# A four-layer image kernel: the first reading in the text's order with spread row transforms, blocks evicted by one engine, logarithms ahead of squares

## The chip, the cores and the metric

The kernel runs on one core of one Trainium2 chip. The metric is the device time of one execution in microseconds (us). Before the change, three executions took 5182.60, 5175.65 and 5182.61 us, the median being 5182.6. One more execution was recorded by the hardware profiler; its own time is in the table below. Engines are named as in the profile: PE is the matrix engine TensorE, DVE is VectorE, ACT is ScalarE, POOL is GpSimd, SP is SyncE, which only issues DMAs here.

## What is computed

An image x of 256 x 256 pixels and 128 channels (float32) goes through four residual layers. Each first normalises x over pixels and groups of four channels:

```
x = x + L0(_gn(x))    # attention along rows, 4 heads of 32, with a pair bias
x = x + L1(_gn(x))    # gated recurrence, 16 steps, with spectra of 7x7 kernels
x = x + L2(_gn(x))    # triangle multiplication
x = x + L3(_gn(x))    # 3x3 convolution, then a dense layer

def _gn(v, G=32, eps=1e-5):
    g = v.reshape(B_, H_, W_, G, C_ // G)
    m = jnp.mean(g, axis=(1, 2, 4), keepdims=True)
    s = jnp.var(g, axis=(1, 2, 4), keepdims=True)
    return ((g - m) / jnp.sqrt(s + eps)).reshape(v.shape)
```

The mean of the first `_gn` is over the whole image, so the image has to be read once before anything else can be done with it. L0 and L2 then apply a layer norm over the channels of each pixel: `(z - mu) * rsqrt(mean((z - mu)**2) + 1e-5)`. L1 needs `fft2` of two sets of 64 complex kernels of 7 x 7, padded to 256 x 256; it is made as a transform of the rows, then of the columns.

## The kernel before

The work is staged layer by layer, on tiles of up to 128 partitions. Three places concern the change.

**The first reading** (`statistics`, L200 to L273). The image is read in 32 blocks of 1 MB. Blocks 6 to 31 come first, through three rotating buffers `xin`; blocks 0 to 5 come last and stay in SBUF as `kept`, for the next stage. Each block has two halves b. For each, DVE subtracts a shift (`xs`, L244), ACT squares the result (`sqx`, L54 for all activations), and PE adds up `xs` and the square of the half before (`add_up`, tile `acc`, four matmuls of 32 columns in four column groups of the array; L60 for all matmuls). `xs` and `sqx` have two buffers each. In between stands work that the statistics do not need: the attention's weights (`attention_weights`, a generator that is advanced twice), and the row transforms of the recurrence's kernels (`kernel_rows`). `spectrum(g)`, called for g = 0 to 15 at blocks 5 to 20, makes eight small matmuls `ph` with 21 rows of weights, and an ACT copy into `H` (L189). After the eighth and the sixteenth call, eight copies `HH<-H` (L196) follow, four on ACT and four on POOL, and two DMAs of 448 KB issued by SP (`HD<-HH`, L197). `H` has one buffer. Here the tile scheduler orders the instructions on each engine; nothing is pinned to the order of the text.

**The turn/normalise loop** (`attention`, L376 to L473), one block of 2048 pixels at a time, every instruction pinned to the text's order (`keep_in_program_order`). `turn(m)` transposes the block in 16 PE transposes, eight for each half, into PSUM tiles `pt`, and copies each half into `xo` (L391 to L393): ACT takes pixels 0 to 3 of each group of eight, DVE pixels 4 to 7. `centre(m, b)` multiplies by the centring matrix (`zc`), adds a bias on DVE (`zs`), squares on ACT (`sq`). `variance(m)` is a mean by PE (`var`), then Ln and Exp on ACT (`rs`). `normalise(m)` spreads `rs` by PE (`pr`), multiplies on DVE, scales on POOL and stores by a POOL DMA. `pair_bias(m)` is a matmul, a DVE copy `bi` and small DMAs. `pt`, `zc` and `pr` share three PSUM buffers.

**The first loop of the triangle** (`triangle`, L1107 to L1149) does the same layer norm on the output of L1, without the turn. Its order is pinned as well. In each iteration: load, `centre(m+1, 0)` with its square, variance of m, `centre(m+1, 1)` with its square, spread, two products on DVE, two POOL instructions, one store. `zc` and `pr` share three PSUM buffers; `zs` and `sq` have four buffers each, `xin` and `zn` three.

All x tiles are loaded by SP, in its order; stores are issued by POOL.

Of the kernel before, what the change touches and what calls it, by code (L numbers as in the profile page):

```python
# [9 lines left out]
F32 = mybir.dt.float32  # L10
AF = mybir.ActivationFunctionType
# [6 lines left out]
P = 128  # L18
# [4 lines left out]
KS = 7  # L23
# [7 lines left out]
class Kernel:  # L31
# [133 lines left out]
    def kernel_rows(self, sp, ps, HD_):  # L165


        nc, I = self.nc, self.i
        CG = HC // 4
        tu = self.load(sp, I["c_rows"], "tu")  # L170
        HH = sp.tile([P, N // 2, HC], F32, name="HH")
        H, ka = [], []
        for n, (re, im) in enumerate((("A_real", "A_imag"), ("B_real", "B_imag"))):
            kr, ki = (I["L1_conv_" + y].rearrange("c p q -> p c q") for y in (re, im))
            k = sp.tile([3 * KS, HC, 32], F32, name=f"ka{n}")
            nc.gpsimd.memset(k, 0.0)
            for p0, q0, src in ((0, 0, kr), (0, KS, ki), (KS, 0, ki), (2 * KS, KS, kr)):
                nc.gpsimd.dma_start(k[p0:p0 + KS, :, q0:q0 + KS], src)
            ka.append(k)

        def spectrum(g):
            n, g0 = divmod(2 * g, CG)
            if not g0:
                H.append(sp.tile([P, N, CG], F32, name="H"))
            ph = ps.tile([P, 2, N], F32, name="ph", bufs=2)
            for j in range(2):
                for k in range(4):
                    self.mm(ph[32 * k:32 * k + 32, j], ka[n][:, CG * k + g0 + j, :], tu)
            nc.scalar.copy(H[n][:, :, g0:g0 + 2].rearrange("q u c -> q c u"), ph)  # L189
            if g0 + 2 == CG:  # L190
                for h in range(2):
                    o = slice(64 * n + 32 * h, 64 * n + 32 * h + 2 * KS)
                    u = slice(h * N // 2, (h + 1) * N // 2)
                    for k in range(4):
                        copy = nc.gpsimd.tensor_copy if h else nc.scalar.copy
                        copy(HH[o, :, CG * k:CG * (k + 1)], H[n][32 * k:32 * k + 2 * KS, u])  # L196
                    nc.sync.dma_start(HD_[n][:, u], HH[o])  # L197
        return spectrum

    def statistics(self, wp, weights, HD_, kept, src):  # L200

        nc, I = self.nc, self.i
        V = nc.vector
        x = I["x"].rearrange("b h w c -> (b h w) c")
        NM, KEPT = NPIX // 2048, len(kept)
        mv = wp.tile([P, 2], F32, name="mvx")
        with ExitStack() as c:
            sp = c.enter_context(self.pool(name="sp", bufs=1))  # L210
            io = c.enter_context(self.pool(name="p0", bufs=2))
            ps = c.enter_context(self.pool(name="p0s", bufs=1, space=PSUM))
            row = sp.tile([1, P], F32, name="row")
            nc.sync.dma_start(row, x[0:1])
            shc = self.column(sp, x[0:1].rearrange("o c -> (o c)"), "shc")
            ones = sp.tile([P, P], F32, name="ones0")
            V.memset(ones, 1.0)
            psh = ps.tile([P, 4, P], F32, name="psh", tag="ph", bufs=2)
            self.mm(psh[:, 0], ones[0:1], row)
            sh = sp.tile([P, P], F32, name="sh")  # L220
            V.tensor_copy(sh, psh[:, 0])
            acc = ps.tile([P, 512], F32, name="acc")
            last, count = None, [0, 0]

            def add_up(*pair):
                for h in range(2):
                    for j, t in enumerate(pair):
                        if t is not None:
                            o = 64 * j + 32 * h
                            self.mm(acc[o:o + 32], ones[:, :32], t[:, h * 512:(h + 1) * 512],  # L230
                                    start=count[j] < 2, stop=count[j] >= 4 * NM - 2)
                            count[j] += 1

            order = list(range(KEPT, NM)) + list(range(KEPT))
            spectrum = None
            for n, m in enumerate(order):
                if m < KEPT:
                    xin = kept[m]
                else:
                    xin = io.tile([P, 2, 1024], F32, name="xin", bufs=3)  # L240
                nc.sync.dma_start(xin, src(m))
                for b in range(2):
                    xs = io.tile([P, 1024], F32, name="xs")
                    V.tensor_tensor(xs.rearrange("p (t c) -> p t c", t=8), xin[:, b].rearrange("p (t c) -> p t c", t=8),  # L244
                                    sh.unsqueeze(1).to_broadcast([P, 8, P]), ALU.subtract)
                    sq = io.tile([P, 1024], F32, name="sqx")
                    self.act(sq, xs, AF.Square)

                    add_up(xs, last)
                    last = sq  # L250
                if n == 2:
                    spectrum = self.kernel_rows(sp, ps, HD_)
                    next(weights)
                elif 5 <= n < 21:
                    spectrum(n - 5)
                elif n == 23:
                    weights = next(weights)
            add_up(None, last)
            accs = sp.tile([P, 512], F32, name="accs")
            V.tensor_copy(accs, acc)  # L260
            sel = sp.tile([P, 2], F32, name="sel")
            V.memset(sel, 0.0)
            V.memset(sel[:64, 0:1], 1.0 / 32 / NPIX)
            V.memset(sel[64:, 1:2], 1.0 / 32 / NPIX)
            pm = ps.tile([P, 2], F32, name="pmx")
            for t in range(4):
                self.mm(pm, accs[:, t * P:(t + 1) * P], sel, start=t == 0, stop=t == 3)
            V.tensor_copy(mv, pm)
            e = sp.tile([P, 1], F32, name="ex")
            V.tensor_tensor(e, mv[:, 0:1], mv[:, 0:1], ALU.mult)  # L270
            V.tensor_tensor(mv[:, 1:2], mv[:, 1:2], e, ALU.subtract)
            V.tensor_tensor(mv[:, 0:1], mv[:, 0:1], shc, ALU.add)
        return mv, weights  # L273
# [59 lines left out]
    def attention(self, wp, later, xT, x1T, znT, biasD, HD_, stats1, shift1):  # L333
# [5 lines left out]
        with ExitStack() as c:  # L339
# [43 lines left out]
            def turn(m):  # L383
                if m >= NM:
                    return
                load(m + 2)
                xo[m] = io.tile([P, 2, P, 8], F32, name="xo")
                for b in range(2):
                    pt = wide("pt").rearrange("c (t p) -> c t p", t=8)
                    for t in range(8):  # L390
                        transpose(pt[:, t], xin[m][:, b, t * P:(t + 1) * P], self.ident)  # L391
                    for h, f in enumerate((acopy, copy)):
                        f(xo[m][:, b, :, 4 * h:4 * h + 4], pt[:, 4 * h:4 * h + 4].rearrange("c t p -> c p t"))  # L393
                nc.gpsimd.dma_start(xT[:, m * 2048:(m + 1) * 2048], xo[m].rearrange("c b p t -> c (b p t)"))

            def centre(m, b):
# [652 lines left out]
    def triangle(self, x2T, x3T, znT, prodD, stats2, shift2, stats3, prepare):  # L1049
# [12 lines left out]
        with ExitStack() as c:  # L1062
# [47 lines left out]
            with ExitStack() as c1:  # L1110
# [10 lines left out]
                def centre(m, b):  # L1121
                    if m >= NB // 2:
                        return
                    zc = ps.tile([P, 1024], F32, name="zc", tag="w")
                    for k in range(2):
                        s = b * 1024 + k * 512
                        mm(zc[:, k * 512:(k + 1) * 512], lc, xin[m][:, s:s + 512])
                    zs[m, b] = work.tile([P, 1024], F32, name="zs")
                    add(zs[m, b], zc, cb)
                    sq[m, b] = work.tile([P, 1024], F32, name="sq")  # L1130
                    act(sq[m, b], zs[m, b], AF.Square)

                table(LN_EXP)
                for m in range(2):
                    load(m)
                centre(0, 0)
                centre(0, 1)
                for m in range(NB // 2):
                    load(m + 2)
                    centre(m + 1, 0)  # L1140
                    rs = variance(ps, work, [sq[m, b] for b in range(2)])
                    centre(m + 1, 1)
                    pr = spreads(ps, rs)
                    zn = io.tile([P, 2048], F32, name="zn")
                    for b in range(2):
                        z = zn[:, b * 1024:(b + 1) * 1024]
                        tt(z, zs[m, b], pr[b], MUL)
                        nc.gpsimd.tensor_scalar(z, z, lnw, lnb, MUL, ADD)
                    nc.gpsimd.dma_start(znT[:, m * 2048:(m + 1) * 2048], zn)  # L1149
# [398 lines left out]
```

## Time and profile before

| what | value |
|---|---|
| time of the profiled execution | 5189.0 us |
| its span | 5187.2 us, 78333 instructions |
| median of the three runs | 5182.6 us |
| PE busy | 4965.6 us (96%) |
| DVE busy | 4108.0 us (79%) |
| ACT busy | 3518.2 us (68%) |
| POOL busy | 427.6 us (8%) |
| mean granted PE clock | 0.983 |
| moved by DMA | 782.5 MB, mean 151 GB/s |
| first reading, to the first `xT` store | 0 to 181.8 us |
| turn/normalise loop | to about 490 us |
| triangle, first loop | 3284 to 3516 us |

The profile gives for each engine how long it was busy, for the span cut in 40 slices how busy (in tenths), and for groups of instructions their number, mean duration and the idle time ahead of them with its releaser. The timeline lists instructions in order of time: start, duration, engine, line, operation, output and inputs, count, and in brackets how long the engine had been idle and what ended that. PEclk is the clock granted to PE as a share of the full one.

### The profile page before, as it was taken

How to read it: one execution, taken by the hardware profiler on the slowest of the kernel's cores; microseconds unless marked ns; L12 is line 12 of the kernel's file. 1: busy time of each engine (PE TensorE's matmuls, PEld its weight loads, DVE VectorE, ACT ScalarE, POOL GpSimd, SP SyncE). 2: the span in 40 equal slices, each digit the busy share in tenths (PEclk: the TensorE clock that was granted, in tenths of full speed). 3: DMA queues.
4: the chain of work that ended last, by engine and by line, in shares of the span. 5: the costliest groups of instructions: out<-in, count | busy, mean ns of one | idle time of the engine just before them, and what ended most of it. 6: DMA issues, size and time to landing. Idle time of an engine off the chain costs nothing.

```text
span 5187.2 us, 78333 instructions
## 1 busy us (share of the span) xinstructions
PE 4965.6 (96%) x31357; PEld 2702.8 (52%) x31357; DVE 4108.0 (79%) x4829; ACT 3518.2 (68%) x4988; POOL 427.6 (8%) x600
## 2 busy tenths in 40 slices
PE   7899999999999899999999999889999989989999
PEld 1343555555555333333333333228999953339999
DVE  4666999999999799999999999665334527779886
ACT  5444888888888799999999999443333347762110
POOL 2132000000000000000000000240110010000000
PEclk7999999999999899999999999999999999999999
DMA  6797222222222222222222221677667768865432
GB/s 192 275 334 264 73 84 78 86 86 82 79 86 86 63 66 71 69 72 67 71 71 66 71 67 66 243 284 268 230 230 255 244 244 333 323 238 188 144 120 66
DMA packets 180093, 782.47 MB, mean 151 GB/s; under 512 B 31696, under 2 KB 35102, under 8 KB 130518
## 3 DMA queue, kind: packets, MB, share of 16 engines
q1 hardware_dynamic: 122366, 508.44, 29.5%
q0 software_dynamic: 56064, 268.58, 13.9%
q8 instruction: 250, 4.10, 0.3%
q14 instruction: 117, 0.96, 0.1%
q10 hardware_dynamic: 1296, 0.40, 0.0%
HBM read 505.99 MB, written 271.32 MB: 150 GB/s over the span
## 4 chain that ended last, share of the span: by engine, by line
PE 53%; DVE 29%; issue 5%; ACT 2%; POOL 0%; DMA 0%; SPq 0%; POOLq 0%; DVEq 0%; ACTq 0%
PE z L60 9%; PE m L60 7%; PE nd L60 7%; PE sc L60 5%; PE po L60 4%; DVE tr L896 3%; DVE t L893 3%; DVE y L893 3%; DVE p L893 3%; DVE yf L893 3%; PE ppq L60 3%; PE ppv L60 2%; PE zc L60 2%; PE px L60 2%; PE pe L60 2%
## 5 line engine op out<-in xcount | busy, mean ns | idle before, releaser
L561 DVE TENSOR_TENSOR e<-sc,bT 128x1024 f32<-128x1024 f32 x512 | 603.1, 1220 | 49.7 <-PE sc L60 48.8
L54 ACT ACTIVATE e<-e 128x1024 f32<-128x1024 f32 x512 | 540.4, 1055 | 61.5 <-DVE e L561 52.4
L1056 DVE TENSOR_TENSOR LR<-z,sg 128x512 f32<-128x512 f32 x256 | 268.2, 1049 | 368.2 <-ACT sg L54 360.4
L60 PE MATMUL m<-U,v 128*128 128x128 f32 x4608 | 517.6, 276 | 6.6 <-DVE v L1397 6.6
L60 PEld LDWEIGHTS m<-U,v 128*128 128x128 f32 x4608 | 517.4, 193 | 6.7 <-DVE v L1397 6.7
L60 PE MATMUL z<-wf,zt 128*128 128x128 f32 x4096 | 461.7, 276 | 4.0 <-DVE LR L1056 2.7
L60 PEld LDWEIGHTS z<-wf,zt 128*128 128x128 f32 x4096 | 461.3, 193 | 5.2 <-DVE LR L1056 2.9
L54 ACT ACTIVATE sq<-zs 128x1024 f32<-128x1024 f32 x192 | 203.0, 1057 | 284.5 <-DVE zs L371 157.7
L54 ACT ACTIVATE sg<-z 128x512 f32<-128x512 f32 x256 | 153.0, 598 | 312.4 <-PE z L60 308.6
L561 DVE TENSOR_TENSOR ks<-e 128x1024 f32<-128x1024 f32 x256 | 301.0, 1217 | 0.0
L60 PE MATMUL sc<-tq,tk 32*128 32x256 f32 x4096 | 297.2, 401 | 2.8 <-DVE e L561 1.9
L60 PE MATMUL nd<-e,tv 128*32 128x256 f32 x4096 | 271.9, 383 | 0.0
L60 PEld LDWEIGHTS sc<-tq,tk 32*128 32x128 f32 x4096 | 186.6, 184 | 159.5 <-issue 96.3
L54 ACT ACTIVATE dn<-dn 128x512 f32<-128x512 f32 x384 | 241.9, 630 | 13.3 <-DVE dn L561 2.6
L60 PE MATMUL av<-y,ident 128*128 128x512 f32 x384 | 192.2, 610 | 44.0 <-DVE y L893 44.0
L60 PE MATMUL po<-LR 128*128 128x256 f32 x1024 | 222.2, 380 | 7.0 <-DVE LR L1056 7.0
L1434 ACT COPY m4s<-m 128x512 f32<-128x512 f32 x32 | 18.7, 585 | 287.3 <-PE m L60 287.3
L60 PEld LDWEIGHTS po<-LR 128*128 128x128 f32 x1024 | 194.1, 190 | 34.2 <-DVE LR L1056 7.7
L60 PE MATMUL bx<-p,ident 128*128 128x512 f32 x384 | 192.3, 610 | 0.0
L54 ACT ACTIVATE o<-po 128x256 f32<-128x256 f32 x256 | 84.3, 381 | 145.3 <-issue 111.6
L60 PEld LDWEIGHTS nd<-e,tv 128*32 128x32 f32 x4096 | 120.2, 110 | 109.8 <-issue 44.2
L864 ACT ACT_TABLE_LOAD x132 | 169.4, 1283 | 1.5
(369 smaller groups left out, 10376.8 us busy)
## 6 DMA issues: line engine op xcount, KB each, us to landing
zt<-znT SPq DMA_DIRECT2D x128, 1024.0 KB
znT<-zn POOLq DMA_DIRECT2D x64, 1024.0 KB, 5.2
xin<-x2T SPq DMA_DIRECT2D x64, 1024.0 KB
xin<-in_x_dram SPq DMA_DIRECT2D x52, 1024.0 KB
xr<-x3T SPq DMA_DIRECT2D x46, 768.0 KB
xT<-xo POOLq DMA_DIRECT2D x32, 1024.0 KB, 8.6
xr<-xT SPq DMA_DIRECT2D x64, 512.0 KB
zn<-znT SPq DMA_DIRECT2D x64, 512.0 KB
```

Source lines behind the costliest of these rows:

```text
L54: return self.nc.scalar.activation(out, in_, func, bias=bias, scale=scale, **kw)
L60: return self.nc.tensor.matmul(out, lhsT, rhs, start=start, stop=stop)
L561: pin = lambda f: lambda *a, **k: tc.keep_in_program_order(f(*a, **k))
L864: pin(nc.scalar.preload_act_table_set(want))
L893: pin(V.tensor_tensor(out, a, b_, op))
L896: pin(V.scalar_tensor_tensor(out, a, k, b_, op0, op1))
L1056: pin = lambda f: lambda *a, **k: tc.keep_in_program_order(f(*a, **k))
L1434: nc.scalar.copy(m4, m[4])
```

## The change

It has three parts. In the first reading, the differences, squares, `acc` and spectrum matmuls and the `H` copies are pinned to the text's order; the weights are asked for after block 1 and block 28, the sixteen spectra are called in two of every three blocks from block 4 on (4, 5, 7, 8, ... 25, 26); all `HH` copies go to POOL, and POOL issues the `HD` writes. In the turn, one engine evicts a whole half: ACT the first, DVE the second. In the triangle's first loop, the square is taken out of `centre` and called after the variance of the block before. As a consequence of the new order, SP issues the six `kept` loads ahead of the last five `xin` loads of the first reading.

```diff
+        pin = lambda f: lambda *a, **k: self.tc.keep_in_program_order(f(*a, **k))
...
-                    self.mm(ph[32 * k:32 * k + 32, j], ka[n][:, CG * k + g0 + j, :], tu)
-            nc.scalar.copy(H[n][:, :, g0:g0 + 2].rearrange("q u c -> q c u"), ph)
+                    pin(self.mm)(ph[32 * k:32 * k + 32, j], ka[n][:, CG * k + g0 + j, :], tu)
+            pin(nc.scalar.copy)(H[n][:, :, g0:g0 + 2].rearrange("q u c -> q c u"), ph)
...
-                        copy = nc.gpsimd.tensor_copy if h else nc.scalar.copy
-                        copy(HH[o, :, CG * k:CG * (k + 1)], H[n][32 * k:32 * k + 2 * KS, u])
-                    nc.sync.dma_start(HD_[n][:, u], HH[o])
+                        nc.gpsimd.tensor_copy(HH[o, :, CG * k:CG * (k + 1)], H[n][32 * k:32 * k + 2 * KS, u])
+                    nc.gpsimd.dma_start(HD_[n][:, u], HH[o])
...
-                            self.mm(acc[o:o + 32], ones[:, :32], t[:, h * 512:(h + 1) * 512],
+                            pin(self.mm)(acc[o:o + 32], ones[:, :32], t[:, h * 512:(h + 1) * 512],
...
-                    V.tensor_tensor(xs.rearrange("p (t c) -> p t c", t=8), xin[:, b].rearrange("p (t c) -> p t c", t=8),
+                    pin(V.tensor_tensor)(xs.rearrange("p (t c) -> p t c", t=8), xin[:, b].rearrange("p (t c) -> p t c", t=8),
                                     sh.unsqueeze(1).to_broadcast([P, 8, P]), ALU.subtract)
...
-                    self.act(sq, xs, AF.Square)
+                    pin(self.act)(sq, xs, AF.Square)
...
-                if n == 2:
+                if n == 1:
                     spectrum = self.kernel_rows(sp, ps, HD_)
                     next(weights)
-                elif 5 <= n < 21:
-                    spectrum(n - 5)
-                elif n == 23:
+                elif n == 28:
                     weights = next(weights)
+                elif n >= 4 and n % 3 and made < 16:
+                    spectrum(made)
+                    made += 1
...
-                    for h, f in enumerate((acopy, copy)):
-                        f(xo[m][:, b, :, 4 * h:4 * h + 4], pt[:, 4 * h:4 * h + 4].rearrange("c t p -> c p t"))
+                    (copy if b else acopy)(xo[m][:, b], pt.rearrange("c t p -> c p t"))
...
-                    sq[m, b] = work.tile([P, 1024], F32, name="sq")
-                    act(sq[m, b], zs[m, b], AF.Square)
+
+                def square(m, b):
+                    if m < NB // 2:
+                        sq[m, b] = work.tile([P, 1024], F32, name="sq")
+                        act(sq[m, b], zs[m, b], AF.Square)
...
-                centre(0, 0)
-                centre(0, 1)
+                for b in range(2):
+                    centre(0, b)
+                    square(0, b)
                 for m in range(NB // 2):
                     load(m + 2)
                     centre(m + 1, 0)
                     rs = variance(ps, work, [sq[m, b] for b in range(2)])
+                    square(m + 1, 0)
                     centre(m + 1, 1)
+                    square(m + 1, 1)
```

More of the change, by code (lines that the diff above doesn't have):

```diff
@@ L222, in statistics @@
             acc = ps.tile([P, 512], F32, name="acc")
+            pin = lambda f: lambda *a, **k: self.tc.keep_in_program_order(f(*a, **k))
             last, count = None, [0, 0]
@@ L234, in statistics @@
             order = list(range(KEPT, NM)) + list(range(KEPT))
-            spectrum = None
+            spectrum, made = None, 0
             for n, m in enumerate(order):
```

## The prediction

> **What bounds the kernel now.** The page's slices come first: the matrix engine (PE) is busy almost everywhere, at nearly full clock, except in the first slices and around slices 25 to 28.
>
> ```profile
> PE   7899999999999899999999999889999989989999
> PEclk7999999999999899999999999999999999999999
> ```
>
> A slice is 129.7 us. The three edited places are the first reading (0 to 181 us), the turn/normalise loop of the attention (181 to 490 us) and the first loop of the triangle (3284 to 3516 us). A profiled span of 5187.2 us holds only some 720 us that the change can touch; the long attention stage, where the chain of waits is all PE, is not touched.
>
> First reading, in the stage table (2 us stages; the columns are PE, PEld, DVE, ACT, POOL busy, PE clock, DMA share, GB/s) and the timeline of DVE:
>
> ```profile
> 62.00:64.00 2.00, 2.00 (x22) 0.70 (x14) 0.94 (x1) 0.51 (x1) 0.00 (x0) 0.50 0.02 8
> 116.00:118.00 2.00, 1.69 (x16) 0.32 (x16) 1.91 (x3) 1.66 (x3) 0.00 (x0) 1.00 1.06 424
> ```
>
> ```profile
> 77.43 2.23 DVE L244 TENSOR_TENSOR xs<-xin,sh 128x1024 f32<-128x1024 f32 x1 [2.53 <-PE acc L60]
> ...
> 98.05 2.36 DVE L244 TENSOR_TENSOR xs<-xin,sh 128x1024 f32<-128x1024 f32 x2 [7.02 <-DMA xin<-in_x_dram]
> 110.28 1.22 DVE L244 TENSOR_TENSOR xs<-xin,sh 128x1024 f32<-128x1024 f32 x1 [9.87 <-ACT sqx L54]
> ...
> 137.96 2.36 DVE L244 TENSOR_TENSOR xs<-xin,sh 128x1024 f32<-128x1024 f32 x2 [8.68 <-DMA xin<-in_x_dram]
> ```
>
> See two things. From 38.25 to 82.75 us the clock is 0.50 and PE is full: seven blocks take 44 us there. After that, three stalls: 7.0 and 8.7 us for x tiles queued in SyncE's ring behind the HD writes (L197), and 9.9 us while ACT does four HH copies in a row. Undisturbed, a block takes 2.45 to 2.55 us (115 to 128 us).
>
> ```profile
> 101.58 7.69 POOL L196 COPY HH<-H 14x2048 f32<-14x2048 f32 x4 [23.00 <-ACT H L189]
> ```
>
> This row prices one POOL copy: 7.69 / 4 = 1.92 us.
>
> Turn/normalise loop, timeline:
>
> ```profile
> 253.21 1.06 ACT L54 ACTIVATE sq<-zs 128x1024 f32<-128x1024 f32 x1 [2.99 <-DVE zs L371]
> ...
> 254.18 1.05 ACT L371 COPY xo<-pt 128x512 f32<-128x512 f32 x2
> ...
> 254.78 1.29 DVE L371 COPY xo<-pt 128x512 f32<-128x512 f32 x2 [1.60 <-ACT xo L371]
> ...
> 255.52 1.98 PE L60 MATMUL zc<-xo,lc 128*128 128x512 f32 x4
> ```
>
> The loop repeats every 9.70 us, and no wait on a DMA is listed. It is a ring: DVE's two zn products, bi copy and zs, ACT's square, ACT's half of xo, then DVE's half of xo (which waits for ACT's half of the same tile), PE's zc, DVE's zs, and round again.
>
> Triangle loop, timeline:
>
> ```profile
> 3412.97 1.28 DVE L1056 TENSOR_SCALAR zs<-zc,cb 128x1024 f32<-128x1024 f32 x1
> 3414.28 1.06 ACT L54 ACTIVATE sq<-zs 128x1024 f32<-128x1024 f32 x1 [3.54 <-DVE zs L1056]
> 3415.25 0.67 ACT L54 ACTIVATE rs<-var,eps 128x512 f32<-128x512 f32 x1
> ...
> 3415.95 0.63 ACT L54 ACTIVATE rs<-rs 128x512 f32<-128x512 f32 x1
> ...
> 3416.63 1.14 PE L60 MATMUL pr<-rs,tspread 32*128 32x512 f32 x8 [1.19 <-ACT rs L54]
> ...
> 3417.86 2.35 DVE L1056 TENSOR_TENSOR zn<-zs,pr 128x1024 f32<-128x1024 f32 x2 [1.04 <-PE pr L60]
> ```
>
> The next zs starts at 3420.13, so the ring is 1.28 + 1.06 + 0.67 + 0.63 + 1.14 + 2.35 = 7.13, measured 7.16 us. The variance needed by the logarithm was ready long before (var 3412.46 to 3413.52); the logarithm stands behind a square that it does not need.
>
> [...] xs takes 1.23 us, and 2.03 and 2.23 us on the two occasions when it fell beside POOL's HH copies. [...]
>
> **First reading, part by part.** The new text pins differences, squares, acc and spectra. Sixteen of the blocks 4 to 26 carry a spectrum, seven do not. Removed: ACT's eight HH copies (8 x 1.90 us), and the HD writes from SyncE's ring, with the 7.0 + 9.9 + 8.7 = 25.6 us of stalls. Added: a ring in each block with a spectrum, because ACT's H copy now stands ahead of the next square and PE's ph ahead of the next acc. At full clock: square 1.02, acc group 0.86, ph 1.15 with its drain, H copy 0.96, handovers 0.16, sum 4.15 us; a plain block 2.4. 16 x 4.15 + 7 x 2.4 = 83 us. At half clock the PE terms double (1.71, 1.86): 6.0 and 3.45 us, 16 x 6.0 + 7 x 3.45 = 120 us.
>
> A new wait: H is one buffer, and all eight copies out of it now run on POOL. The ninth H copy (block 16) comes 5.6 us after the eighth, while POOL needs 8 x 1.92 + 0.6 for the DMA issue + about 2.2 beside xs = 18.3 us. ACT stalls about 12.7 us with all later squares behind it, and with them acc and xs. The second set runs beside blocks 27 to 31: xs at 2.13 instead of 1.23 us, so a block takes 4.26 and five of them 20 us. POOL issues the HD writes; nothing else of POOL's is due before the first xT store. The six kept loads, now ahead of five xin loads in SyncE's order, take 6 x 2.56 = 15.4 us of transfer, hidden by the ACT stall. The first xo has to wait for the last HD write: POOL ends near 158, the write lasts perhaps 5 us, the first xo is due near 168; covered, by 5 us.
>
> Timeline at full clock: block 4 at 40 us as before, + 83 + 12.7 + 3 for a clock dip in that stall = 139; + 20 = 159 us for the last square, against 169.7 now: -11 us. At half clock throughout: about 190, +20 us. A spectrum block at full clock holds 1.72 us of acc in 4.15[...]. I take a quarter of the distance: **-3 us**, ends -13 and +20.
>
> **Evictions.** ACT's half of xo ended at 254.77 and DVE's first half at 255.47. One ACT copy of 1024: 0.58 for 512 plus 0.46 for the rest (the slope from sg's 0.598 to sq's 1.057 us on the page), 1.04 us from 254.18: 255.22, so zc starts 0.25 us earlier. DVE's own tile (about 1.22, as L692's 1024 copy) fits in its idle time of 253.2 to 254.8. The rest of the ring is unchanged: 31 x 0.25 = **-8 us**; ends 0 (DMA share is already 0.94 to 0.96 here) and -9. [...]
>
> **Triangle.** With logarithm and exponential ahead of the squares the old ring opens. Next is PSUM: three wide buffers, four uses a block, so zc of the next block waits for the zs that empties the second zc. From the rows: zc 1.92 to issue, var 0.99, zc to the end 2.09, zs 1.28, handover 0.06: 6.34 us. DVE's sum (1.28 x 2 + 2.35 = 4.9) and ACT's (3.4) are less. DMA: 2.10 MB a block at the 342 GB/s reached in the other loop is 6.1 us, just below. (7.16 - 6.34) x 30 = **-25 us**; ends -34 (6.04) and -12 (6.75, if DMA binds).
>
> Sum: -3 - 8 - 25 = -36 us. The profiled execution took 5189.0 us (span 5187.2 plus 1.8); it would take 5153. The median of the runs is 6.4 us lower, so 5182.6 - 36 = **5147 us**.
>
> **The rivals.** *Half clock in the first reading*: for it, the 44 us at 0.50[...]. +20 - 8 - 25 = -13: 5170. *DMA takes the gains of both loops*: for it, the shares; against, no listed DMA wait. -3 + 0 - 10 = -13: 5170. *All rings shorter than worked out* (clock never falls, triangle at 6.0): -11 - 8 - 34: 5130. *Slower: the triangle goes serial.* If var or its logarithm had to await the previous zn, the ring would be zs, sq, var, Ln, Exp, pr, zn and the other zs: 1.28 + 1.06 + 1.06 + 0.67 + 0.63 + 1.14 + 2.35 + 1.28 = 9.5 us, 30 x 2.3 = +70; with the others +59: 5242. Against it: zs and sq have four buffers each. It decides the sign from a period of 7.5 us up.
>
> **Chances.** Forecast (5138 to 5158) 0.62; half clock 0.14; DMA 0.10; shorter 0.09; serial 0.05. About 0.2%, 10 us, is what a measurement of this kernel can tell. Faster takes 0.62 + 0.09 + most of the two at -13 (0.16) = 0.87; same 0.07; slower 0.06. The range reaches to 5126 below and 5172 above, which takes in both cases at 5170 and most of the shorter one.
>
> **What would show it.** Right: triangle blocks every 6.3 us, with zc waiting for zs; the loop before every 9.45 us; one ACT wait of 10 to 15 us on POOL at the ninth H copy; xs near 2.1 us in the last five blocks; first xo at 165 to 175 us. Wrong: a clock of 0.50 through most of 40 to 130 us, a first xo after 185, DMA waits in either loop, or a triangle period of 7 us or more.

## The result, and the profile after

| | before | after |
|---|---|---|
| median of 13 runs | 5179.8 us (5172.5 to 5193.4) | 5162.5 us (5155.0 to 5170.6) |
| ratio after / before | | 0.9964, 95% interval 0.9956 to 0.9973 |
| profiled execution (span) | 5189.0 us (5187.2) | 5160.9 us (5159.1) |

The change saves 18.6 us by the ratio (14 to 23 by its interval), where 36 were forecast. The profiled pair differs by 28.1 us, 9.5 more than the ratio. Where the pair's 28 us lie is read from a few marks that both traces have (start times, us):

| mark | before | after | difference |
|---|---|---|---|
| first `xs` | 23.36 | 18.19 | -5.2 |
| `accs` (sums of the first reading) | 170.83 | 166.10 | -4.7 |
| first `xT` store | 181.79 | 177.50 | -4.3 |
| first `sc` matmul (attention proper) | 507.96 | 495.79 | -12.2 |
| last `x1T` store | 1748.14 | 1739.88 | -8.3 |
| first `zc` of the triangle | 3284.01 | 3276.14 | -7.9 |
| first `LR` (next triangle stage) | 3524.89 | 3497.90 | -27.0 |
| end of the span | 5187.2 | 5159.1 | -28.1 |

So the first reading itself gained nothing: from the first `xs` to the sums it took 147.5 us before and 147.9 after. The turn/normalise loop gave 7.9, of which 3.9 came back in the attention, and the triangle gave 19.1.

The page's slices of after, to be set against the two shown of before: in PE the second slice (first reading) and the 27th (triangle) went from 8 to 9; the clock changed in the first two only.

```profile
PE   7999999999999899999999999899999989989999
PEclk8899999999999899999999999999999999999999
```

The stage table of after for the two stages shown of before, and two that are new (columns as there, POOL busy ahead of the clock):

```profile
62.00:64.00 2.00, 1.92 (x14) 0.37 (x10) 0.42 (x1) 1.85 (x3) 0.00 (x0) 1.00 0.72 213
116.00:118.00 2.00, 1.28 (x8) 0.34 (x12) 1.80 (x2) 1.06 (x1) 0.00 (x0) 0.50 0.74 299
86.00:88.00 2.00, 1.21 (x2) 0.00 (x0) 0.00 (x0) 0.00 (x0) 1.96 (x3) 0.50 0.82 201
152.00:154.00 2.00, 1.11 (x12) 0.07 (x8) 2.00 (x2) 0.23 (x2) 1.96 (x3) 0.50 1.56 180
```

At 62 us, among the spectra, the clock is 1.00 (it was 0.50). At 116 us it is 0.50, behind a wait for an x tile. At 86 us POOL alone works steadily, at 152 us POOL and DVE, and the clock is 0.50 too. The timeline of DVE, POOL and ACT in after shows what they wait for there:

```profile
60.01 2.42 DVE L224 TENSOR_TENSOR xs<-xin,sh 128x1024 f32<-128x1024 f32 x2 [1.62 <-ACT sqx L54]
...
74.61 10.63 DVE L224 TENSOR_TENSOR xs<-xin,sh 128x1024 f32<-128x1024 f32 x4 [1.63 <-ACT sqx L54]
95.20 1.23 DVE L224 TENSOR_TENSOR xs<-xin,sh 128x1024 f32<-128x1024 f32 x1 [9.96 <-ACT sqx L54]
...
115.44 2.36 DVE L224 TENSOR_TENSOR xs<-xin,sh 128x1024 f32<-128x1024 f32 x2 [8.36 <-DMA xin<-in_x_dram]
...
140.42 21.94 DVE L224 TENSOR_TENSOR xs<-kept,sh 128x1024 f32<-128x1024 f32 x8 [1.63 <-ACT sqx L54]
```

```profile
73.79 13.20 POOL L197 COPY HH<-H 14x2048 f32<-14x2048 f32 x5 [62.99 <-ACT H L181]
...
153.30 7.99 POOL L197 COPY HH<-H 14x2048 f32<-14x2048 f32 x3
```

```profile
93.31 1.01 ACT L181 COPY H<-ph 128x512 f32<-128x512 f32 x1 [12.57 <-POOL HH L197]
```

Three costs stand here. ACT waits 12.57 us for POOL's eighth copy, so DVE stands 9.96 us. An x tile comes 8.36 us late. And `xs` takes 10.63 / 4 = 2.66 and 21.94 / 8 = 2.74 us beside POOL's copies, against 1.21 alone; a POOL copy takes 13.20 / 5 = 2.64, against 1.92.

The turn/normalise loop of after, one turn of the ring:

```profile
251.10 1.28 DVE L374 TENSOR_SCALAR zs<-zc,cb 128x1024 f32<-128x1024 f32 x1 [2.65 <-PE zc L60]
...
256.77 1.22 DVE L374 COPY xo<-pt 128x1024 f32<-128x1024 f32 x1 [0.33 <-PE pt L374]
257.44 0.99 ACT L374 COPY xo<-pt 128x1024 f32<-128x1024 f32 x1
258.56 1.98 PE L60 MATMUL zc<-xo,lc 128*128 128x512 f32 x4
...
260.64 1.28 DVE L374 TENSOR_SCALAR zs<-zc,cb 128x1024 f32<-128x1024 f32 x1 [2.65 <-PE zc L60]
```

ACT's whole half ends at 258.43 and `zc` starts 0.13 us later. From this `zs` to the same one of the next block it is 9.54 us, against 9.70, and most blocks of the loop keep that period.

The triangle's first loop of after:

```profile
3391.30 1.28 DVE L1058 TENSOR_SCALAR zs<-zc,cb 128x1024 f32<-128x1024 f32 x1
...
3392.23 0.69 ACT L54 ACTIVATE rs<-var,eps 128x512 f32<-128x512 f32 x1 [2.01 <-PE var L60]
3392.95 0.63 ACT L54 ACTIVATE rs<-rs 128x512 f32<-128x512 f32 x1
3393.49 1.04 ACT L54 ACTIVATE sq<-zs 128x1024 f32<-128x1024 f32 x1
...
3395.51 1.98 PE L60 MATMUL zc<-xin,lc 128*128 128x512 f32 x4 [0.36 <-DVE zs L1058]
...
3397.63 1.28 DVE L1058 TENSOR_SCALAR zs<-zc,cb 128x1024 f32<-128x1024 f32 x1
```

The logarithm no longer stands behind a square, and `zc` waits for the `zs` that empties its PSUM buffer: the new ring, with a period of 3397.63 - 3391.30 = 6.33 us.

### The profile page after: what moved, and what is told of

It reads as the page before. It is cut to its first block, busy times and chain, and to the rows that moved or that the text cites. A ratio compares the mean times of both kernels' runs of the same rounds, so it can differ in the third digit from the quotient of the medians.

```text
span 5159.1 us, 78300 instructions
## 1 busy us (share of the span) xinstructions
PE 4960.6 (96%) x31357; PEld 2701.3 (52%) x31357; DVE 4119.8 (80%) x4797; ACT 3497.7 (68%) x4948; POOL 451.8 (9%) x612
## 4 chain that ended last, share of the span: by engine, by line
PE 55%; DVE 28%; issue 5%; ACT 1%; DMA 1%; POOL 0%; SPq 0%; POOLq 0%; DVEq 0%; ACTq 0%
PE z L60 9%; PE m L60 7%; PE nd L60 7%; PE sc L60 5%; PE zc L60 4%; PE po L60 4%; DVE tr L898 3%; DVE t L895 3%; DVE y L895 3%; DVE p L895 3%; DVE yf L895 3%; PE ppq L60 3%; PE ppv L60 2%; PE px L60 2%; PE pe L60 2%
```

## The experiments

All times are medians, set against runs of the kernel before on the same chip. "First xs to sums" is the time from the first `xs` to `accs` in the profile; it leaves out a start that varies (see the section on the hardware).

| kernel | median us | ratio to before (95%) | first xs to sums |
|---|---|---|---|
| before | 5179.8 | 1 | 147.5 |
| after | 5162.5 | 0.9964 (0.9956 to 0.9973) | 147.9 |
| first part alone | 5190.0 | 1.0017 (1.0010 to 1.0023) | 148.8 |
| evictions alone | 5177.2 | 0.9990 (0.9982 to 0.9997) | 137.3 |
| logarithms alone | 5156.8 | 0.9952 (0.9938 to 0.9966) | 137.4 |
| after, zt behind x | 5154.2 | 0.9946 (0.9934 to 0.9959) | 147.6 |
| that without the first part | 5151.0 | 0.9946 (0.9933 to 0.9958) | 148.9 |
| after, x loads chained | 5162.3 | 0.9961 (0.9947 to 0.9975) | 148.8 |
| after, all loads chained | 5155.1 | 0.9959 (0.9943 to 0.9974) | 141.1 |
| after, two H | 5154.5 | 0.9948 (0.9932 to 0.9965) | 139.2 |
| after, half the copies on ACT | 5148.1 | 0.9940 (0.9925 to 0.9956) | 137.2 |
| after, shift from PSUM | 5140.1 | 0.9924 (0.9908 to 0.9941) | 127.7 |
| all mended | 5128.8 | 0.9903 (0.9886 to 0.9919) | 115.2 |
| all mended, m first | 5129.2 | 0.9906 (0.9893 to 0.9919) | 118.7 |

My theory after the result was that each part keeps what the marks give it: 4 us, 8 us and 18 to 19 us. The rival: one of the parts is negative, and the profiled pair hides it.

### Each part alone

Edit of the first: only `statistics` and `kernel_rows` as after, all else as before.

> The first part alone (first reading in the text's order, spread spectra, HH copies and HD writes on POOL), on the kernel before. Theory, from the two traces: the first xo and the first xT store come 4 us earlier (store near 177.5 instead of 181.8 us), nothing later moves, so 5180 - 4 = 5176 us, ratio 0.9992. Rival: what the attention gives back (the marks of the changed kernel lose 4 us between its first and last stores) comes from this part, then the ratio is 1.000 or above. ACT's wait for POOL at the ninth H copy should again be 12 to 13 us and the wait for an x tile near 115 us again about 8 us, since neither needs the other two parts.

Measured: 5190.0 us against 5180.3, **9.6 us slower** (5 to 12 by the interval). ACT's wait is 12.58 us again. My theory fell: the first part is a loss, and the 4.3 us of the first marks are none of its doing, since they lie ahead of the first `xs`, which here starts at 22.80 us. The rival's reason fell too: from the first `sc` to the last `x1T` this kernel takes 1240.2 us like before, so the loss is not in the attention.

> The second part alone (a whole half of the turn evicted by one engine), on the kernel before. Theory: the period of the turn/normalise loop is 9.54 us instead of 9.70, 31 times 0.16 = 5 us, and up to 3 us more at the loop's ends: 5172 to 5175 us, ratio 0.9985 to 0.9990. As predicted blind (period 9.45) it would be -8 us, 0.9985. Rival: the gain needs the first part as well (other tiles kept, other state of the queues), then the period stays at 9.70 and the ratio is 1.000.

Measured: -3.1 us (-9 to -2). From the first `xT` store to the last the loop takes 291.0 us instead of 297.7, 6.6 less, and 7.9 less to the first `sc`. From there to the last `x1T` it takes 1244.0 us instead of 1240.2: half of the gain comes back, as it did in the whole change. (The next kernel, whose turn is the old one, takes 1241.8 us there, so not all of that belongs to this edit.)

```diff
-                    for h, f in enumerate((acopy, copy)):
-                        f(xo[m][:, b, :, 4 * h:4 * h + 4], pt[:, 4 * h:4 * h + 4].rearrange("c t p -> c p t"))
+                    (copy if b else acopy)(xo[m][:, b], pt.rearrange("c t p -> c p t"))
```

> The third part alone (squares of the triangle's first loop behind the variance of the block before), on the kernel before. Theory: the period is 6.33 us with three or four longer ones while SP fetches five zt tiles among the x tiles; the loop is 18 us shorter and the end of the kernel 17 to 18 us earlier: 5162 us, ratio 0.9966. That would make this part nearly the whole gain of the change. Rival: the medians of the whole change are only 18.6 us apart and the two traces 28, so this part may carry only 10 to 12 us (0.998) if the blocks of the loop meet a slower DMA without the other parts.

Measured: -23.5 us (-32 to -18); in the trace 221.7 us from the first `zc` to the first `LR`, against 240.9 before, -19.2. The rival fell. The three parts add up to +9.6 - 3.1 - 23.5 = -17.0, the whole to -18.6. One part carries nearly all of the gain, and another takes a third of it away.

These last two kernels have the old first reading, and show what the profile of before could not: its 147.5 us is not what this code always takes. One 4 us stage of three executions of the same first reading (before; logarithms alone; the later kernel without the first part):

```profile
60.00:64.00 4.00, 4.00 (x30) 0.95 (x22) 1.29 (x2) 0.51 (x1) 0.00 (x0) 0.50 0.17 70
```

```profile
60.00:64.00 4.00, 3.49 (x34) 0.75 (x32) 0.75 (x2) 3.97 (x4) 3.01 (x2) 1.00 0.80 275
```

```profile
60.00:64.00 4.00, 4.00 (x28) 1.01 (x24) 1.99 (x2) 1.65 (x2) 0.00 (x0) 0.50 0.59 231
```

In two of the four profiles with the old first reading the clock stands at 0.50 for over 40 us and the reading takes 147.5 and 148.9 us; in the other two the reading takes 137.3 and 137.4. Of these, logarithms alone has 0.50 from 40 to 44 us like before, but 1.00 from 60 to 64; the mean clock of its execution is 0.985, that of evictions alone too, where the two with the long stretch have 0.983 and 0.982. Both with the low clock were long executions of their kernels (5189.0 among 5172 to 5193, and 5158.7, the longest of six). The new reading takes 147.6 to 148.8 us in the three profiles of it as it stands (after, first part alone, zt behind x) and in the one with the x loads chained; in after and in the last one the clock is 1.00 until POOL's first set. So the first part is worth about +11 us against the executions of 137 us and nothing against the others.

The other runs bear this out, since each has its mean clock on record; 44 us at 0.50 take 22 / 5187 = 0.004 from it. Of the 62 runs of before beside the experiments, 14 have 0.982 or 0.983, the other 48 have 0.985 or 0.986, and none lies between. In the set of 43 beside the first part alone the first kind averages 5190.0 us and the second 5178.2. The first part alone, at 0.984 or 0.985 in all 21 runs, averages 5190.2: the same as before with the low clock, and 12 us above before without it, which is the more frequent. So the two profiles with the low clock were no accident of profiling, and the median of before is a run without it.

### Where the first part loses: four repairs

```diff
-                H.append(sp.tile([P, N, CG], F32, name="H"))
+                H.append(sp.tile([P, N, CG], F32, name=f"H{n}"))
```

(For room, the two padded kernels `ka` share one tile with a pitch of 14 instead of 32; each matmul still reads 32 columns, and rows 14 to 31 of each group of 32 in `H`, which nobody copies, hold other channels' values instead of zeros.)

> The changed kernel with H in two buffers (the two padded kernels share one narrower tile to make room; the same matmuls). ACT's ninth H copy then needs no POOL copy, so its wait of 12.57 us goes. Theory: little of it reaches the end, because two other things take its place: xs goes on at 2.8 us beside POOL's copies, and the x tile behind the six kept loads now comes late by more than the 8.36 us of the changed kernel. Gain 3 to 5 us, last square 4 us earlier counted from the first xs. Rival: the ACT wait is what sets the end: 12 us earlier. The first xs itself starts anywhere from 18 to 24 us, since DVE stands behind a weight's DMA at the start; so stages are counted from it.

Measured: 139.2 us to the sums, 8.7 less. ACT's wait is gone, but `xs` stays slow beside POOL for longer:

```profile
80.80 23.08 DVE L227 TENSOR_TENSOR xs<-xin,sh 128x1024 f32<-128x1024 f32 x9 [1.64 <-ACT sqx L54]
```

The edit also let SyncE issue the x tiles in a better order, by the scheduler's doing, so the late x tile is gone as well: against the kernel with that repair alone (141.1, below), two buffers give 1.9 us. The theory's sum was too small because it expected the late tile to grow; its point, that little of the 12.57 us reaches the end, holds.

```diff
-                nc.sync.dma_start(xin, src(m))
+                self.chain("x", nc.sync.dma_start(xin, src(m)))
```

> The changed kernel with the x loads of the first reading issued in the order of the blocks, so that no kept load stands ahead of an earlier block's. Theory: the wait of 8.36 us for an x tile near 115 us goes and nothing takes its place, the kept tiles coming at 2.6 us each while blocks take 5: 8 us from the first xs to the sums. Rival: the kept loads, now issued when the last xin buffer is free near 135 us, share the DMA with the last HD write and stall DVE there by as much: no gain.

Measured: no gain, and a wait of 9.09 us for the same tile:

```profile
121.53 2.36 DVE L224 TENSOR_TENSOR xs<-xin,sh 128x1024 f32<-128x1024 f32 x2 [9.09 <-DMA xin<-in_x_dram]
```

The theory missed; the rival has its "no gain", but not for its reason. SyncE's timeline shows 24 small weight loads in the place that the kept loads had left, from 91.65 to 114.05 us, two pairs of them held for over 5 us while an HD write was under way:

```profile
94.19 5.69 SPq L325 DMA_DIRECT2D rbi<-in_L_conv_bi_dram  x2
...
100.58 5.92 SPq L325 DMA_DIRECT2D rbd<-in_L_conv_bd_dram  x2
...
114.05 14.14 SPq L243 DMA_DIRECT2D xin<-in_x_dram  x5
```

So the edit was repeated with every load of that queue chained (`self.load`, `self.column`, the `rb` and `ev` loads too); no other engine's order moves.

> The changed kernel with all loads that SyncE issues in the first reading in the text's order: 24 x loads without a break, then the six kept ones, then the later weights (before, pinning the x loads alone had let 24 small weight loads slip in at the place of the kept ones). The other engines' orders are unchanged. Theory: the x tile near 115 us comes in time, the wait of 8.36 us goes, and the first xs to the sums takes 140 us instead of 148. Rival: it is the two HD writes[...] and not the loads ahead that hold the x tile: a wait of 5 us or more stays there.

Measured: the wait is gone, 141.1 us to the sums, 6.8 less than after. The timeline of DVE at that place (the second row is the block that came late):

```profile
103.77 2.36 DVE L224 TENSOR_TENSOR xs<-xin,sh 128x1024 f32<-128x1024 f32 x2 [0.47 <-PE acc L60]
107.58 2.42 DVE L224 TENSOR_TENSOR xs<-xin,sh 128x1024 f32<-128x1024 f32 x2 [1.45 <-ACT sqx L54]
```

That settles it for the loads that stand ahead of the tile, and against the HD writes as such.

```diff
-            psh = ps.tile([P, 4, P], F32, name="psh", tag="ph", bufs=2)
+            psh = ps.tile([P, 4, P], F32, name="psh")
...
-            sh = sp.tile([P, P], F32, name="sh")
-            V.tensor_copy(sh, psh[:, 0])
...
-                                    sh.unsqueeze(1).to_broadcast([P, 8, P]), ALU.subtract)
+                                    psh[:, 0].unsqueeze(1).to_broadcast([P, 8, P]), ALU.subtract)
```

> The changed kernel with xs reading the shift from its PSUM tile instead of a copy in SBUF, so that xs has one SBUF input. Theory: xs no longer contends with POOL's HH copies; beside them it takes 1.25 instead of 2.83 us, and a copy 1.92 instead of 2.65. At the first set the ACT wait becomes longer in place of it (POOL is done 3 us earlier, so 3 us net), at the second set the last four blocks take 10 us instead of 22: 12 to 15 us in all from the first xs to the sums. Rival: the slow xs comes from something else than the second SBUF input (POOL's traffic as such): xs stays near 2.8 us, no gain.

Measured: 22 us less than after in the medians, 20.2 less to the sums, more than expected. The same places in this kernel's timeline:

```profile
134.81 9.80 DVE L222 TENSOR_TENSOR xs<-kept,psh 128x1024 f32<-128x1024 f32 x8 [1.64 <-ACT sqx L54]
```

```profile
133.99 9.62 POOL L197 COPY HH<-H 14x2048 f32<-14x2048 f32 x5 [42.70 <-ACT H L181]
```

`xs` takes 1.22 us beside POOL instead of 2.74, a POOL copy 1.92 instead of 2.64. So the slow `xs` came with the shift's copy in SBUF, and not with POOL's traffic as such, which the rival named. From the last eight `xs` to the sums it is 12.1 us instead of 25.7 (-13.6); the rest comes at the first set, which ends 3.8 us earlier, and at the x tile (6.60 instead of 8.36 us late).

```diff
-                        nc.gpsimd.tensor_copy(HH[o, :, CG * k:CG * (k + 1)], H[n][32 * k:32 * k + 2 * KS, u])
+                        copy = nc.gpsimd.tensor_copy if h else nc.scalar.copy
+                        copy(HH[o, :, CG * k:CG * (k + 1)], H[n][32 * k:32 * k + 2 * KS, u])
```

> The changed kernel with four of the eight HH copies of each set back on ACT, as before the change; pins, spread and POOL's HD writes stay. Theory: POOL is done with its four in 8 to 11 us, so ACT's wait for it is gone or short, but ACT itself is busy 7.6 us with copies that its squares wait for: 4 to 8 us gained at the first set. At the second set only half as many xs fall beside POOL (6 us gained) and the squares wait 7.6 us (lost): nothing. From the first xs to the sums 140 to 144 us instead of 148. Rival: the copies' place doesn't matter, ACT's 15 us of copies are lost whole: 148 us or more.

Measured: 137.2 us to the sums, 10.7 less, beyond the theory's 4 to 8. The two engines copy side by side:

```profile
73.76 7.66 POOL L198 COPY HH<-H 14x2048 f32<-14x2048 f32 x4 [62.98 <-ACT H L181]
```

```profile
73.73 7.62 ACT L198 COPY HH<-H 14x2048 f32<-14x2048 f32 x4
```

No `xs` falls beside POOL now, because the squares stand behind ACT's copies and DVE stands with them (9.51 and 9.50 us): both engines are done in 7.6 us, where POOL alone needed 19.5 and 21.7. The scheduler's order of loads differs too (only two kept loads ahead; an x tile 5.46 us late instead of 8.36), so some 3 us of the 10.7 are not the copies'. The old split of the copies was the better one. The 137.2 us are also what the old reading takes without the long stretch at 0.50 (137.3 and 137.4): with the old split the rest of the part, late x tile included, neither gains nor loses against that. The pins and the spread by themselves were not run.

### The triangle's rest, and the best kernel

```diff
-                        nc.sync.dma_start(xin[m], x2T[:, m * 2048:(m + 1) * 2048])
+                        self.tc.keep_in_program_order(nc.sync.dma_start(xin[m], x2T[:, m * 2048:(m + 1) * 2048]))
...
-                            nc.sync.dma_start(zt, znT[:, b * 1024:(b + 2) * 1024])
+                            self.tc.keep_in_program_order(nc.sync.dma_start(zt, znT[:, b * 1024:(b + 2) * 1024]))
```

> The changed kernel with one more edit: in the triangle SP issues all x tiles of the first loop ahead of the first zt tile (the loads pinned in the text's order). Theory: the three long periods (7.51, 9.70 and 6.70 us instead of 6.33, together 4.9 us) come from five zt loads that share the DMA with x loads and znT stores and stand ahead of x tiles; without them all 31 periods are 6.33 us and the loop is 5 us shorter, ratio to the kernel before 0.9954 against 0.9964 of the changed kernel. Rival: the zt tiles are then not there when the next stage starts, which gives 3 to 5 us back at its start: ratio 0.9964, with the first LR later by that much after the last znT store. Second rival: the long periods are the x loads' own, at 2.1 MB in 6.33 us, and stay.

The stores of after, with the long periods, and those of this kernel in the same stretch:

```profile
3325.18 0.57 POOL L1157 DMA_DIRECT2D znT<-zn  x1 [0.30 <-POOL zn L1156]
3331.51 0.57 POOL L1157 DMA_DIRECT2D znT<-zn  x1 [0.30 <-POOL zn L1156]
3339.02 0.57 POOL L1157 DMA_DIRECT2D znT<-zn  x1 [0.30 <-POOL zn L1156]
3348.72 0.57 POOL L1157 DMA_DIRECT2D znT<-zn  x1 [0.30 <-POOL zn L1156]
```

```profile
3327.97 0.57 POOL L1157 DMA_DIRECT2D znT<-zn  x1 [0.30 <-POOL zn L1156]
3334.31 0.57 POOL L1157 DMA_DIRECT2D znT<-zn  x1 [0.30 <-POOL zn L1156]
3340.63 0.57 POOL L1157 DMA_DIRECT2D znT<-zn  x1 [0.30 <-POOL zn L1156]
3346.97 0.57 POOL L1157 DMA_DIRECT2D znT<-zn  x1 [0.30 <-POOL zn L1156]
```

The periods of 7.51 and 9.70 us are gone; a third long one, of 6.70 us, is still there later in the loop, so the zt loads were not its cause. The stretch from the first `zc` to the last store is 3.6 us shorter, and the first `LR` still follows the last store after 4.56 us (4.59): the zt tiles were wanted no earlier. The theory held for two of its three long periods.

> The first reading as before the change; evictions, logarithms and the zt loads behind the x loads as in the best kernels so far. Theory: the three add up to -3.1 - 23.5 - 3 = -30 us (the two parts measured alone, and 3.6 us between the znT stores of the triangle), ratio 0.9943, so that leaving the first part out beats the whole change by about 10 us; from the first xs to the sums it takes 137 us, as in the two other kernels with the old first reading, against 148 to 149 with the first part. Rival: the first part was slow alone only because of what the old turn loop does behind it; then this kernel is no faster than the changed one, 0.9964. Second possibility: the clock stands at 0.50 from 38 to 83 us as in the profile of the kernel before; then 147 us to the sums in this profile.

Measured: 0.9946, 28 us below before, near the 30 that the parts add up to. But it equals the kernel with the first part (0.9946; each interval is 0.0025 wide), so this pair doesn't confirm the 10 us; and its profile is one with the low clock (148.9 us, the second possibility). The isolated run says +9.6 (5 to 12), this pair 0, give or take 9. I take a loss of 5 to 10 us.

> The changed kernel with all four: H in two buffers, x loads in order, shift from PSUM, zt loads behind the x loads in the triangle. Theory: sixteen blocks at 4.05 us and sixteen at 2.4 us with no wait in between, 104 to 115 us from the first xs to the sums instead of 148, and 3 us in the triangle: 33 + 3 us below the changed kernel, ratio to the kernel before 0.989 to 0.991. Rival: something else is late next (the last HD write ahead of the first xo, which is written where H lay; or the clock at one half), then half of it: 0.993.

Measured: **5128.8 us, ratio 0.9903 (0.9886 to 0.9919)**, 33.6 us below after in the medians, the best kernel of the study. To the sums it takes 115.2 us, 32.8 less. Shift and order alone gave 20.2 + 6.8; that leaves 5.8 for the second H, worth 1.9 while `xs` was slow, if the three simply add up, which no run separates. (Here the chain on the x loads alone is enough: no small load slips in among them.) Two waits remain, as the rival had it but small: an x tile (2.98 us) and the first `xo`, which the trace shows waiting for the last HD write:

```profile
147.38 1.01 ACT L375 COPY xo<-pt 128x1024 f32<-128x1024 f32 x1 [3.41 <-DMA HD<-HH]
```

> All mended (two H, x in order, shift from PSUM, zt behind x) and one more edit: the load of the block matrix m, for which DVE stands with the first xs behind it, issued first on ACT's queue. Theory: the first xs starts at 12 to 15 us instead of 18 to 24, everything else shifts with it: 5120 to 5123 us, ratio 0.989. Rival: the x tile or another weight is late next, and the first xs still starts at 18 us or later: 0.9903 as before.

Measured: the rival. The first `xs` still starts at 23.47 us: with `m` early, another weight of that queue is late:

```profile
16.63 0.28 DVE L304 TENSOR_SCALAR wg<-rawg,lns 128x128 f32<-128x128 f32 x1 [7.45 <-DMA rawg<-in_L_conv_Wg_dram]
```

## Why the prediction was half right

The sign and the range held; the sum was twice what came. At 5162.5 us the median lies between the main case (5138 to 5158) and the two rivals at 5170, and neither rival came about: the clock stayed up between the spectra (1.00 until 84.0 us), and both loops took the periods of their rings, but for 3.6 us in the triangle that the next stage's loads cost (below).

**Triangle, -25: right.** The period is 6.33 (forecast 6.34), by the ring that was worked out, with `zc` waiting for `zs`. The trace gives -19.1, the part alone -23.5. Of the missing 5.5 us in the trace 3.6 are the zt loads (the prefetch of the next stage) among the x loads. The prediction had bounded this ("if DMA binds"), but from the loop's own bytes, not from a prefetch of the next stage that rides in the same queue.

**Evictions, -8: mechanism right, size off.** The period is 9.54, not 9.45: `zc` follows ACT's copy after 0.13 us, where the prediction kept the 0.05 us that it had followed DVE's. 31 x 0.16 is 5 us; the loop gave 6.6, the rest at its first blocks. That the attention behind it then takes 1.2 to 3.9 us more (first `sc` to last `x1T`, in every kernel but the first part alone, and so in logarithms alone too, whose turn is the old one) was in no step; where it comes from stays open.

**First reading, -3: the wrong step.** It failed as "block 4 at 40 us as before ... for the last square, against 169.7 now". The 169.7 us belongs to an execution with 44 us of half clock, which the same code doesn't have every time; against the others the new reading is 11 us longer. The ends of -13 and +20 held the +9.6 that the part measured alone, but the middle was reckoned from an execution at the long end. Against that same execution -3 looks good (147.9 us to the sums, 147.5 before), but by luck: the clock did better than forecast, which alone would have made it -11, and the late x tile and the slow `xs` took that away. Its details, by their own steps:
- Spectrum blocks: 4.05 us, forecast 4.15. Up to POOL's first set the clock did not fall in any of them. That it would fall in some (+8 us) was the author's estimate, and what makes it fall or return is not shown by any run. The trace of after has 2.75 to 3.51 us of `acc` in each 4 us from 40 to 76 us. The clock fell in the two waits instead, from 84.0 to 104.5 and from 114.7 to 121.5 us, where 3 us had been set aside.
- ACT's wait at the ninth H copy: 12.57 us, forecast 12.7.
- Last blocks: `xs` beside POOL at 2.74 us, forecast 2.13. The forecast took two single meetings of an `xs` with a POOL copy (2.03 and 2.23 us); in a row of eight each takes longer. With POOL at 2.64 instead of 1.92, the last four blocks take 25.7 us to the sums; the kernel with the shift in PSUM needs 12.1. (The forecast's own five blocks of 4.26 us are 21.3, not 20.)
- "The six kept loads ... hidden by the ACT stall": not hidden. The wait for x was 8.36 us, and removing what stands ahead gave 6.8.
- The first `xo` came at 174 us, in the band of 165 to 175, but 5.2 us of that come from a first `xs` that happened to start earlier.
- The case of half clock was reckoned too long: its terms (1.02, 1.71, 1.86, 0.96, 0.16) give 5.71 us for a block with a spectrum, not 6.0, and 115 us instead of 120 in all. It did not come about.

**Profiled time against the median.** The prediction made its sum on one execution and carried the difference over to the median as it stood. That assumes that the execution is long everywhere alike. It was long in the first reading: the pair's 28.1 us hold 5.2 us of an earlier first `xs`, and some 10 us of low clock in before. Without the start the pair differs by 23, without both by 13; the medians lie between, at 18.6.

## What to carry to other kernels

Before a gain is reckoned against a stage of one profiled execution, ask which of its numbers would differ in the next one: a clock at 0.50 in a stage with dense work is such a number (44 us of it in two of four profiles here), and a second profile of the same code shows it. When copies move to an idle engine, count what that engine does to the instructions that run beside it in a row, and what stands behind the first buffer that it now holds; here half the copies on each engine gave 10.7 us to the sums and one operand in PSUM 20.2, each more than the 9.6 us that the part lost. A load queue is an order: take one transfer out of its place, and look at what slips in.

## What the runs showed of the hardware

- The clock of one and the same code: in two of four profiles 0.50 for 44.4 us (38.4 to 82.8 us in before, 34.1 to 78.5 us in the later kernel without the first part), and 147.5 and 148.9 us to the sums; in the other two 137.3 and 137.4. In before PE was busy for all of the 44.4 us, in each 4 us from 40 to 80 us with 1.59 to 3.64 us of `acc`; the clock came back in a stretch (80 to 84 us) with 3.81 us of `acc` and no `ph`. What sets the clock was not shown: no run changed `acc` or `ph` alone.
- With `acc` matmuls between the small ones (2.75 to 3.51 us of `acc` in each 4 us from 40 to 76 us in after) the clock stayed at 1.00 from 40 us to POOL's first set in after and in the seven repairs of its first reading (x loads chained, all loads chained, two H, half the copies on ACT, shift from PSUM, and both kernels with all mended).
- In the last blocks of after eight `xs` (1.21 us each alone) and eight POOL copies (1.92) end within 22.8 us, from 139.60 to 162.36; one after the other they would take 25.0. So each takes longer beside the other (2.74 and 2.64 us), and still they overlap in part.
- The first `xs` started at 15.3 to 24.0 us with nearly the same instructions ahead of it on DVE. In before DVE stands ahead of it for two weights, 5.16 us for `wo` and 4.08 us for `m`, while x tiles of 1 MB are under way (DMA share 1.06, 102 GB/s from 11 to 16 us); with the load of `m` first, DVE stood 7.45 us for `rawg`.
- An HD write of 448 KB goes as 14 packets of 32 KB that start within 0.4 us and take up to 5.1 us each: 5.2 us in after (153.83 to 159.04), 88 GB/s. A stretch of 4 us that holds all their starts lists a share of 1.01 and 115 GB/s (153 to 157 us in after). While x tiles are loaded, after lists 410 GB/s (24 to 26 us).
